# Conv-attention megakernel: the Fourier step's order in layer 0, and the last image's feed-forward with layer 1's norm behind it and its last group in halves

## The chip, the cores and the metric

The kernel runs on one core of one Trainium2 chip. The core has five engines, each with a queue of its own that is worked off in order: PE (TensorE, matmuls into PSUM), ACT (ScalarE), DVE (VectorE), POOL (GpSimd) and SP, which here only issues DMAs. The time is device microseconds of one execution; the number compared is the median of several executions. Lower is better.

## The reference

Eight images of 256 channels and 32 x 32 pixels, all float32, go through two layers. Layer 0 is a convolutional attention block followed by a feed-forward with a Fourier filter; layer 1 treats the pixels as 1024 tokens: causal attention, then eight experts with dense gates. Only the parts that the change touches are shown.

```python
def _edffn(x, pi_w, dw_w, fft_p, po_w):          # layer 0's feed-forward
    x = _conv1x1(x, pi_w)                        # 256 -> 1024 channels
    x = _dwconv3(x, dw_w)                        # 3 x 3 taps per channel
    x1, x2 = (x[:, :hid], x[:, hid:])            # hid = 512
    x = gelu(x1) * x2
    x = _conv1x1(x, po_w)                        # 512 -> 256 channels
    xp = x.reshape(B, Cc, gh, PS, gw, PS).transpose(0, 1, 2, 4, 3, 5)   # 8 x 8 blocks
    xf = jnp.fft.rfft2(xp) * fft_p
    xp = jnp.fft.irfft2(xf, s=(PS, PS))
    return xp.transpose(0, 1, 2, 4, 3, 5).reshape(B, Cc, Hp, Wp)

def _forward(x, ...):                            # layer 0
    a = _attention(_ln(x, norm1_w, norm1_b), ...)
    x = x + gamma1 * a
    f = _edffn(_ln(x, norm2_w, norm2_b), pi_w, dw_w, fft_p, po_w)
    return x + gamma2 * f

t = t + _L1_attn_ref(_ln_t(t), WQ, WK, WV)       # layer 1, attention
t = t + _L1_ffn_ref(_ln_t(t), ...)               # layer 1, experts
```

## The kernel before

Channels lie on the 128 partitions, so an image is two channel groups of 1024 pixels. All instructions of layer 0 and layer 1 go through recorders (class `InOrder`, line 73 in the profile's rows) that keep each engine's queue in the order in which the Python code issues them. Nothing is reordered later: what stands early in an engine's queue and is not ready holds up what stands behind it. Only the DMAs issued with `nc.sync` are free.

**Layer 0 is staggered over the images.** While image i's attention runs (`main_of(i)`, mostly PE and ACT), the taps of the feed-forward of image i-1 run on DVE (`hidden(i-1, ...)`), and at the opening of `main_of(i)` image i-2 gets its Fourier step (`spectrum(i-2)`). The function `level` weaves the two by costs: after each yield of the main list it issues side steps, in the main taps of 128 x 1024, until the summed DVE cost reaches a share of the summed PE cost (0.95 for images 2 to 6, 1.05 for image 7). The first 16 side steps of an image are the taps `o` of its own position encoding (`v_conv`), for which ACT first writes the middle tap (`v_middle`).

**The Fourier step** works on four bands of 256 pixels. For each band, `first` mixes 512 channels to 256 on PE (`pz`, eight matmuls that the profile counts as sixteen, since each is done in two passes) and ACT copies the result (`zf`); `second` is the product with the Fourier basis (`pf`) and, on DVE, the filter (`gf`); `third` is the product back (`py`) and two DVE additions into the image (`t`). I number them by band: pz 0, pf 0, gf 0, py 0, t 0 and so on; the two halves of the norm's output are xn 0 and xn 1. Before, a round of the loop issues `first(n)`, then `second(n-1)`, then `third(n-2)`, with a yield after each.

**The norm before the feed-forward** (`norm2`, `rms_norm`) is woven into that step: squares on ACT, their sums on PE (`ms`), the level on ACT (`yr`), a transpose (`tpy`), the factors on POOL, five empty steps, a transpose back (`tr`, then ACT's `rT`), and for each half a product that spreads the factors (`rbn`) and two DVE products (`xn`). `xn` is the input of the next group's opening `ph`. Then come the attention's scores `s` (product, ACT's `pT`, products `po` and `sums`).

The PSUM tiles `ms`, `tpy`, `tr`, `rbn`, `pf`, `py`, `pp` and `ph` share two banks (`ps_m`, tag `mm`); a new tile waits until an older one has been read.

**The last image** has no attention beside it. After `main_of(7)` the code runs, by hand order: the Fourier step of image 6 with the rest of image 7's attention (`ends`, `project`, product `pp`) and norm, woven with layer 1's first norm of image 0 (`norm0`, function `layer_norm`: transposes `tpt`, statistics on DVE, a chain on POOL, scalings of `zt_e` on ACT, transposes back `tpz`, copies `z_e`). Then the feed-forward of image 7 (`hidden(7, (), (2,), alone=True)`): eight channel groups of 128, of which group 2 runs its taps as products on PE (`pc`) and seven run them on DVE, eight taps each besides ACT's middle one. Groups 0 to 3 (`x`) go through gelu and are multiplied with groups 4 to 7 (`conv`) to `hid`; each such product is mixed at once (`mix`, into four `pz` tiles held over the whole image). Beside it, weighted by `together`, run 26 empty steps (`LEAD`) and then layer 1's keys and values of image 0 (`pk`, `pv`). At the end `spectrum(7)` runs alone, and layer 1 begins with the scores `s<-kk_e,z_e`.

Of the kernel before, what the change touches and what calls it, by code (L numbers as in the profile page):

```python
# [18 lines left out]
P = 128  # L19
# [7 lines left out]
PS = 8  # L27
# [78 lines left out]
def conv_attn_hybrid_kernel(  # L106
# [471 lines left out]
    with ExitStack() as l0:  # L578
# [484 lines left out]
        def hidden(b, lead, on_pe=(), alone=False):  # L1063


            opening = cur = None
            on_dve = [n for n in range(2 * ng) if n not in on_pe]
            for i, us in enumerate(lead):
                if opening is None and i >= 6 and b in ready2:
                    opening = open_group(b, 0, hpad[0])  # L1070
                    cur = next(opening)
                    next(opening)
                    opened = i
                elif opening is not None and i == opened + 2:
                    next(opening)

                yield us
            while b not in ready2:
                yield None
            if opening is None:  # L1080
                opening = open_group(b, 0, hpad[0])
                cur = next(opening)
                next(opening)
                opened = 16
            if opened > 13:
                next(opening)
            hid = hid_of[b] = {"h": {}, "out": [], "gelu": 0, "alone": alone}
            others = [(g, 3 * i) for i, g in enumerate(on_pe)]
            beside = {}
            for g, at in others:  # L1090

                beside[at + 1, 1], beside[at + 1, 6], beside[at + 2, 6] = g, g, g
            running = {}
            for m, n in enumerate(on_dve):
                pad, dst = cur
                for i, k in enumerate(OTHERS):
                    if m + 1 < len(on_dve):
                        if i == 3:
                            opening = open_group(b, on_dve[m + 1], hpad[(m + 1) % 2])
                            cur = next(opening)  # L1100
                            next(opening)
                        if i == 5:
                            next(opening)
                    if (m, i) in beside:
                        g = beside[m, i]
                        if g not in running:
                            running[g] = group_on_pe(b, g)
                        next(running[g])
                    tap(dst, pad, dw_w[:, n, :], k)
                    yield 1.3  # L1110
                hid["h"][n] = dst
                complete(b)

        def complete(b):

# [26 lines left out]
                gate(b)  # L1142
                yield 0.0

        def mix(b, g):

            pzs = mixed.setdefault(b, [])
            if not pzs:
                pzs += [ps_s.tile([P, 2, 2, C], F32, tag="s", name="pz") for _ in range(2)]
            for n in range(4):  # L1150
                for k in range(2):
                    blk = hid_of[b]["out"][g][:, (2 * n + k) * P : (2 * n + k + 1) * P]

                    pe.matmul(
                        pzs[n // 2][:, n % 2, k, :], blk, pow_[:, g, :], start=(g == 0 and k == 0), stop=(g == ng - 1 and k == 1)
                    )
# [3 lines left out]
        def spectrum(b):  # L1160

            hid = hid_of[b]["out"]
            nb = H // PS

            def first(n):
                if b in mixed:
                    pz = mixed[b][n // 2][:, n % 2]
                    z = two.tile([P, 2, C], F32, tag="ev", name="zf", bufs=3)
                    act.copy(z, pz)
                    return z  # L1170
                pz = ps_s.tile([P, 2, C], F32, tag="s", name="pz")
                for k in range(2):
                    for g in range(ng):
                        blk = hid[g][:, (2 * n + k) * P : (2 * n + k + 1) * P]
                        pe.matmul(pz[:, k, :], blk, pow_[:, g, :], start=(g == 0), stop=(g == ng - 1))
                z = two.tile([P, 2, C], F32, tag="ev", name="zf", bufs=3)
                act.copy(z, pz)
                return z

            def second(z):  # L1180
                pf = ps_m.tile([P, 2, C], F32, tag="mm", name="pf")
                pe.matmul(pf, dft, z, start=True, stop=True)
                gf = two.tile([P, 2, C], F32, tag="ev", name="gf", bufs=3)
                dve.tensor_mul(gf, pf, filt.unsqueeze(1).to_broadcast([P, 2, C]))
                return gf

            def third(n, gf):
                py = ps_m.tile([P, KC, PS, 2, W // 2], F32, tag="mm", name="py")
                for g in range(KC):
                    for k in range(2):  # L1190
                        pe.matmul(py[:, g, :, k, :], gf[:, k, g * P : (g + 1) * P], idft, start=True, stop=True)
                for g in range(KC):
                    tb = t[b][:, g, n * BAND : (n + 1) * BAND]
                    dve.scalar_tensor_tensor(
                        tb, py[:, g].rearrange("p r k c -> p (r k c)"), col("gam2", g), tb, ALU.mult, ALU.add
                    )

            z, gf = {}, {}
            for n in range(nb + 2):
                if n < nb:  # L1200
                    z[n] = first(n)
                    yield 3.5
                if 1 <= n <= nb:
                    gf[n - 1] = second(z.pop(n - 1))
                    yield 0.9
                if n >= 2:
                    third(n - 2, gf.pop(n - 2))
                    yield 0.9
            nc.sync.dma_start(t_d[b], t[b])
            if b + 3 < B:  # L1210
                load_x(b + 3)
# [16 lines left out]
        def silent(steps, n=None):  # L1228
            for _ in itertools.islice(steps, n):
                pass  # L1230
# [9 lines left out]
        def main_of(i):  # L1240

            steps = attend(i)
            if i >= 1:
                if i == 1:
                    second = norm2(i - 1)
                    silent(steps, 1)
                    silent(project(i - 1, (1,)))  # L1250
                    silent(second, 2)
                    v_middle(i)
                    yield from weave(second, steps, 2, rest=False)
                else:
                    mixing, second = spectrum(i - 2), norm2(i - 1, 5)
                    silent(second, 1)
                    silent(mixing, 1)
                    silent(project(i - 1, (1,)))
                    silent(second, 1)
                    v_middle(i)  # L1260
                    yield from some(mixing, 1)
                    yield from some(second, 1)
                    yield from some(mixing, 1)
                    yield from weave(second, mixing, 1, rest=False)
                    yield from weave(mixing, steps, 2, rest=False)
            yield from weave(steps, later_on(3, queries_keys(i + 1)) if 1 <= i < B - 1 else none(), 1)
            gelus = gelu_steps(i - 1) if i >= 1 else none()
            if i + 1 < B:
                stack(i + 1)
                steps, ends = values(i + 1), finish(i)  # L1270
                yield from some(gelus, 2)
                yield from some(steps, 2)
                yield from gelus
                yield from some(ends, 1)
                yield from project(i, (0,))
                yield from some(steps, 2)
                yield from some(ends, 1)
                yield from some(steps, 1)
                yield from ends
                yield from steps  # L1280
            else:
                yield from gelus
                yield from some(finish(i), 1)
                yield from project(i, (0,))
# [69 lines left out]
        silent(ends)  # L1354
        silent(mixing, 2)
        silent(project(B - 1, (1,)))
        head = weave(weave(second, mixing, 1), norm0, 1)
        while not ready2.get(B - 1):
            next(head)

        def rest():
            yield from head
            yield from itertools.repeat(1.0, LEAD)
            for us in keys0:
                yield 2.5 * us

        together(rest(), hidden(B - 1, (), (2,), alone=True), 1.0)
        for _ in spectrum(B - 1):
            pass


# [698 lines left out]
```

## Time and profile before

| | before |
|---|---|
| median of three executions | 3064.48 us (3064.29 to 3064.49) |
| profiled execution: time | 3065.18 us |
| profiled execution: span | 3063.5 us |
| PE busy | 2913.9 us (95%) |
| DVE busy | 2339.7 us (76%) |
| ACT busy | 1621.6 us (53%) |
| POOL busy | 317.1 us (10%) |
| mean granted clock of PE | 0.979 |
| layer 1's first scores | at 1353.46 us |

The span is that of the profiled execution, from its first to its last instruction. A row of the timeline gives start, duration, engine, line, operation, output and inputs, the number of merged instructions, and in square brackets the idle time of that engine just before and what ended it. A row of the windows gives the stretch, its length, and for PE, PE's weight loads, DVE, ACT and POOL the busy time with the number of instructions; then the granted clock of PE (1.00 is full), the DMA share and GB/s. A row of the waits gives who waited for whom, the total in us, the number of times and the longest.

### The profile page before, as it was taken

The numbers are of one execution on the slowest core, as the hardware profiler recorded it, in microseconds if no ns is written. First come the engines' busy times: TensorE is split into PE (matmuls) and PEld (weight loads), VectorE is DVE, ScalarE is ACT, GpSimd is POOL, SyncE is SP. The second block draws the span as 40 slices with busy tenths as digits, with TensorE's granted clock in tenths as the row PEclk, the third lists the DMA queues.
The fourth block names the chain that finished last, engine by engine and source line by source line (L and its number), as shares of the span: only waits on it lengthen the run. The fifth ranks groups of instructions, "written<-read, shape, count | busy, mean of one in ns | idle before, by whom it ended". The sixth has DMA issues, their size and how long they took to land.

```text
span 3063.5 us, 41588 instructions
## 1 busy us (share of the span) xinstructions
PE 2913.9 (95%) x16802; PEld 1923.7 (63%) x16802; DVE 2339.7 (76%) x2886; ACT 1621.6 (53%) x2440; POOL 317.1 (10%) x453
## 2 busy tenths in 40 slices
PE   7989999999999989889999999999999999999998
PEld 4644655555555555456666666677777777777775
DVE  2378888888888878776566654688988988888887
ACT  2555554545454535434444443565666666666664
POOL 1011111111111110011222222000000000000000
PEclk8999999999999989999999999999999999999999
DMA  6203030303030301003333311421211251122210
GB/s 196 48 10 83 28 84 28 83 29 83 29 83 29 83 15 35 16 35 128 131 133 122 126 78 69 165 83 49 90 69 69 97 186 69 69 76 90 76 69 29
DMA packets 63856, 234.87 MB, mean 77 GB/s; under 512 B 5590, under 2 KB 13862, under 8 KB 54822
## 3 DMA queue, kind: packets, MB, share of 16 engines
q1 hardware_dynamic: 63654, 232.12, 23.1%
q8 instruction: 134, 2.20, 0.3%
q14 instruction: 68, 0.56, 0.1%
HBM read 140.61 MB, written 91.49 MB: 76 GB/s over the span
## 4 chain that ended last, share of the span: by engine, by line
PE 74%; DVE 14%; ACT 6%; POOL 2%; DMA 2%; issue 2%; SPq 0%; ACTq 0%; DVEq 0%; POOLq 0%
PE pm L73 12%; PE pa L73 11%; PE q L73 11%; PE po L73 9%; PE s L73 6%; PE ph L73 6%; PE pq L73 3%; DVE conv L73 3%; PE sums L73 3%; DVE o L73 3%; DVE x L73 2%; ACT zt_e L73 2%; PE pz L73 2%; PE pv L73 2%; PE pp L73 2%
## 5 line engine op out<-in xcount | busy, mean ns | idle before, releaser
L73 PE MATMUL pa<-ze,w 128*128 128x512 f32 x1488 | 423.2, 393 | 0.0
L73 DVE SCALAR_TENSOR_TENSOR x<-hpad,vec,x 128x1024 f32<-128x1024 f32 x248 | 316.8, 1283 | 68.4 <-ACT x L73 60.9
L73 DVE SCALAR_TENSOR_TENSOR conv<-hpad,vec,conv 128x1024 f32<-128x1024 f32 x256 | 327.4, 1283 | 9.7 <-ACT conv L73 3.6
L73 PEld LDWEIGHTS pa<-ze,w 128*128 128x128 f32 x1488 | 278.4, 188 | 63.3 <-issue 3.3
L73 ACT ACTIVATE h<-pa,bn_o,s1a 128x512 f32<-128x512 f32 x256 | 198.6, 776 | 202.1 <-PE pa L73 202.1
L73 ACT ACTIVATE pT<-s 128x1024 f32<-128x1024 f32 x256 | 247.6, 1024 | 84.4 <-PE s L73 84.3
L73 PE MATMUL po<-pT,vT 128*32 128x256 f32 x4096 | 271.9, 383 | 0.0
L73 PE MATMUL q<-h2p,w 128*128 128x512 f32 x768 | 270.1, 460 | 0.1
L73 DVE SCALAR_TENSOR_TENSOR h<-pa,s1b,h 128x512 f32<-128x512 f32 x256 | 191.6, 748 | 96.4 <-PE pa L73 87.7
L73 PE MATMUL ph<-xn,piw 128*128 128x512 f32 x512 | 238.9, 608 | 13.4 <-ACT vpad L73 6.9
L73 PE MATMUL pm<-h,w 128*128 128x512 f32 x512 | 242.0, 595 | 0.0
L73 PE MATMUL q<-z_first,w 128*128 128x512 f32 x768 | 216.0, 390 | 2.8 <-DVE z_first L73 1.7
L73 PE MATMUL pm<-h1p,w 128*128 128x512 f32 x768 | 216.1, 389 | 0.5 <-DVE h1p L73 0.5
L73 PEld LDWEIGHTS q<-h2p,w 128*128 128x128 f32 x768 | 144.8, 189 | 84.3 <-issue 60.1
L73 DVE SCALAR_TENSOR_TENSOR o<-vpad,pe_w,o 128x1024 f32<-128x1024 f32 x128 | 164.0, 1283 | 26.1 <-ACT o L73 22.9
L73 PE MATMUL s<-qst,kst 128*128 128x256 f32 x1024 | 172.2, 311 | 8.9 <-ACT pT L73 6.3
L73 PEld LDWEIGHTS po<-pT,vT 128*32 128x32 f32 x4096 | 120.1, 110 | 84.4 <-issue 2.8
L73 PEld LDWEIGHTS ph<-xn,piw 128*128 128x128 f32 x512 | 92.3, 192 | 127.5 <-issue 99.5
L73 PEld LDWEIGHTS q<-z_first,w 128*128 128x128 f32 x768 | 143.8, 188 | 34.1 <-DVE z_first L73 2.9
L73 PEld LDWEIGHTS s<-qst,kst 128*128 128x128 f32 x1024 | 136.3, 193 | 45.2 <-issue 28.8
L73 PEld LDWEIGHTS pm<-h1p,w 128*128 128x128 f32 x768 | 144.1, 188 | 31.6 <-DVE h1p L73 0.9
L73 PE MATMUL sums<-pT,ones 128*32 128x256 f32 x2048 | 157.6, 379 | 0.0
(281 smaller groups left out, 5105.8 us busy)
## 6 DMA issues: line engine op xcount, KB each, us to landing
ze<-zd SPq DMA_DIRECT2D x29, 1536.0 KB, 6.4
qst<-part SPq DMA_DIRECT2D x32, 512.0 KB, 9.5
kst<-part SPq DMA_DIRECT2D x32, 512.0 KB, 16.4
te<-ud SPq DMA_DIRECT2D x32, 512.0 KB, 4.1
wd<-parts_w SPq DMA_DIRECT2D x20, 768.0 KB, 3.7
w<-wd SPq DMA_DIRECT2D x20, 768.0 KB, 5.7
zd<-parts SPq DMA_DIRECT2D x14, 1024.0 KB, 3.8
ud<-te SPq DMA_DIRECT2D x18, 512.0 KB, 3.4
```

Of the source, the lines that this page charges most:

```text
L73: return self._tc.keep_in_program_order(method(*args, **kwargs))
```

## The change

Three edits, all in layer 0's function body.

In `spectrum`, a round of the loop issues `second(n-1)` ahead of `first(n)`, and in `main_of(i)` for images 2 to 7 one more step of that list (now the product and filter of band 0) is taken without a yield, behind the norm's first sums and ahead of `v_middle`.

In the last image, only the first 12 of the 18 steps of `norm0` are woven into the head; the six that scale and transpose back follow at the start of `rest`, after the feed-forward's first group has been opened and its first tap issued by `next(feed)`. `LEAD`'s empty steps, keys and values follow behind them.

The last DVE group of the last image goes through the new `last_group`: its taps, products and mixing run on pixels 0 to 511 and then on 512 to 1023, and four steps of the image's Fourier step (bands 0 and 1: copy, product, filter) are issued between the taps of the second half. `mix` gets an argument for the halves.

```diff
@@ hidden @@
             for m, n in enumerate(on_dve):
                 pad, dst = cur
+                if alone and m == len(on_dve) - 1:
+                    yield from last_group(b, n, pad, dst)
+                    break
                 for i, k in enumerate(OTHERS):
...
+        def last_group(b, n, pad, dst):
+
+
+            hid, g, nb = hid_of[b], n - ng, H // PS // 2
+            assert len(hid["out"]) == g == ng - 1 and hid["gelu"] == ng
+            prod = two.tile([P, N], F32, tag="hid", name="hid", bufs=ng + 1)
+            hid["out"].append(prod)
+            blocks = prod.rearrange("p (n r k c) -> p k n r c", r=PS, k=2, c=W // 2)
+            a, b2 = (x.rearrange("p (n r k c) -> p k n r c", r=PS, k=2, c=W // 2) for x in (hid["h"][g], dst))
+            for h in range(2):
+                part = dst[:, h * HALF : (h + 1) * HALF]
+                for i, k in enumerate(OTHERS):
+                    src = inside(pad, h * (H // 2) + k // 3, k % 3, H // 2)
+                    dve.scalar_tensor_tensor(rows(part), src, dw_w[:, n, k : k + 1], rows(part), ALU.mult, ALU.add)
+                    if h == 1 and i in (1, 2, 4, 6):
+                        next(ending)
+                    yield 0.7
+                ns = slice(h * nb, (h + 1) * nb)
+                for k in range(2):
+                    dve.tensor_mul(blocks[:, k, ns], a[:, k, ns], b2[:, k, ns])
+                mix(b, g, (h,))
...
-        def mix(b, g):
+        def mix(b, g, halves=(0, 1)):
...
-            for n in range(4):
+            for n in (2 * h + i for h in halves for i in range(2)):
@@ spectrum @@
             for n in range(nb + 2):
+                if 1 <= n <= nb:
+                    gf[n - 1] = second(z.pop(n - 1))
+                    yield 0.9
                 if n < nb:
                     z[n] = first(n)
                     yield 3.5
-                if 1 <= n <= nb:
-                    gf[n - 1] = second(z.pop(n - 1))
-                    yield 0.9
                 if n >= 2:
                     third(n - 2, gf.pop(n - 2))
                     yield 0.9
@@ main_of @@
                     silent(mixing, 1)
                     silent(project(i - 1, (1,)))
                     silent(second, 1)
+                    silent(mixing, 1)
                     v_middle(i)
@@ behind the loop over the images @@
-        head = weave(weave(second, mixing, 1), norm0, 1)
+        head = weave(weave(second, mixing, 1), some(norm0, 12), 1)
         while not ready2.get(B - 1):
-            next(head)
+            next(head, None)
+        feed = hidden(B - 1, (), (2,), alone=True)
+        next(feed)
 
         def rest():
             yield from head
+            yield from norm0
             yield from itertools.repeat(1.0, LEAD)
             for us in keys0:
                 yield 2.5 * us
 
-        together(rest(), hidden(B - 1, (), (2,), alone=True), 1.0)
-        for _ in spectrum(B - 1):
+        ending = spectrum(B - 1)
+        together(rest(), feed, 1.0)
+        for _ in ending:
             pass
```

More of the change, by code (lines that the diff above doesn't have):

```diff
@@ L1112, in hidden @@
                 complete(b)
+        def last_group(b, n, pad, dst):
[3 more added lines that the diff above has]
+            hid["out"].append(prod)
+            blocks = prod.rearrange("p (n k r c) -> p k n r c", r=PS, k=2, c=W // 2)
+            a, b2 = (x.rearrange("p (n r k c) -> p k n r c", r=PS, k=2, c=W // 2) for x in (hid["h"][g], dst))
[11 more added lines that the diff above has]
+                mix(b, g, (h,))
         def complete(b):
```

## The prediction

> **What bounds the kernel now.** I read the page first, then TensorE's waits in layer 0, then the order of time of one image's opening and of the last image.
>
> ```profile
> PE 74%; DVE 14%; ACT 6%; POOL 2%; DMA 2%; issue 2%; SPq 0%; ACTq 0%; DVEq 0%; POOLq 0%
> ```
>
> The chain that ended last is three quarters TensorE: time given back to PE counts unless another engine holds the same stretch. TensorE's waits between 150 and 1320 us are led by the wait that the edit aims at:
>
> ```profile
> PE py L73 <- DVE gf L73: 24.0, 11, 4.8
> ```
>
> Is it PE's time to win? Here is VectorE, then PE, at the opening of image 4 (images 2 to 6 are alike):
>
> ```profile
> 617.01 10.53 DVE L73 SCALAR_TENSOR_TENSOR o<-vpad,pe_w,o 128x1024 f32<-128x1024 f32 x8 [2.05 <-ACT o L73]
> 627.46 0.68 DVE L73 TENSOR_TENSOR gf<-pf,filt 128x512 f32<-128x512 f32 x1
> 628.06 3.92 DVE L73 SCALAR_TENSOR_TENSOR o<-vpad,pe_w,o 128x1024 f32<-128x1024 f32 x3
> 631.89 0.68 DVE L73 TENSOR_TENSOR gf<-pf,filt 128x512 f32<-128x512 f32 x1
> 632.49 0.87 DVE L73 SCALAR_TENSOR_TENSOR t<-py,vec,t 128x256 f32<-128x256 f32 x2
> 633.28 2.60 DVE L73 SCALAR_TENSOR_TENSOR o<-vpad,pe_w,o 128x1024 f32<-128x1024 f32 x2
> ...
> 638.09 0.87 DVE L73 SCALAR_TENSOR_TENSOR t<-py,vec,t 128x256 f32<-128x256 f32 x2
> ```
>
> ```profile
> 623.54 1.02 PE L73 MATMUL pf<-zf,dft 128*128 128x512 f32 x2
> 628.20 2.08 PE L73 MATMUL py<-idft,gf 128*128 128x128 f32 x8 [3.64 <-DVE gf L73]
> 630.07 5.32 PE L73 MATMUL pz<-pow__152,hid 128*128 128x256 f32 x16
> ...
> 637.13 0.38 PE L73 MATMUL tr<-ident,r 128*8 128x128 f32 x2
> ...
> 642.97 1.20 PE L73 MATMUL s<-qst,kst 128*128 128x256 f32 x8
> ```
>
> The reader is to see that VectorE idles under 0.6 us from 617.01 until the last xn (start 641.94): 14 taps of 1.31 (8, 3, 2 and 1), four gf of 0.6, the t and xn pairs. PE waits 3.64 us because gf stands behind eight taps, yet it reaches s only when VectorE has worked through the list. The wait is cover for a chain on VectorE. The gap also costs clock; the granted clock (third figure from the end) in stretches of 3.41 us:
>
> ```profile
> 623.30:626.71 3.41, 1.26 (x4) 0.38 (x2) 3.30 (x4) 0.58 (x1) 3.16 (x4) 1.00 0.00 0
> 626.71:630.12 3.41, 1.92 (x9) 1.92 (x10) 3.38 (x4) 0.00 (x0) 1.28 (x3) 0.50 0.00 0
> 776.90:780.31 3.41, 1.38 (x5) 0.50 (x3) 3.30 (x4) 0.58 (x1) 3.16 (x4) 1.00 0.00 0
> ```
>
> Image 5 had the same gap and kept its clock (last line): from its first tap to s it took 25.45 us, image 4 took 25.96. So half clock cost only 0.5 there.
>
> **Images 2 to 6.** No instruction is added. The extra silent step puts pf 0 before pz 1, and its gf before all taps: PE 615.1 to 616.0, gf 616.2 to 616.8, inside the 2.05 us in which VectorE waits for ACT's middle taps anyway. That takes 0.6 from VectorE's chain; without the cover it would be late by 0.6. The pacing (costs written in the code) still emits 14 taps before the last xn, now as 8, 3, 3: gf0, 8 taps, gf1, 3 taps, t0, gf2, 3 taps, t1, gf3, t2, xn, t3, xn. Two things move against it. (1) PE runs pf 3 ahead of tr. PSUM has two banks for these tiles, so the third in the row py 1, pf 3, tr waits for t1, and behind tr stand the rest of the row and s. (2) Both t2 and t3 now stand ahead of the xn that followed them, and t2 must wait for a py that PE can start only after gf3; before, xn 0 filled that time.
>
> By the rows: gf1 at 627.46, t0 at 631.89, gf2 at 632.7, three taps, t1 at 637.1. PE: pf 1 at 620.4, pz 2 to 624.9, py 0 to 625.9, wait 2.3 for gf1, pf 2, pz 3 to 632.5, py 1, pf 3 to 634.8, then 3.4 us idle until t1 gives its bank back at 638.1 (1.02 after its start). At full clock: py 2 at 638.65, t2 639.75, xn 640.55, py 3 640.8, last rbn 642.1, s 642.5: 0.45 earlier than 642.97. At half clock (py pair to t 2.12 instead of 1.10, rbn to xn 1.15 instead of 0.69, as at 1103 us in image 7): t2 640.8, xn 641.7, py 3 641.8, last rbn 643.7, s 644.5: 1.5 later, and s to po takes 3.9 (334.90 to 338.79) instead of 3.4: +2.0.
>
> Which clock? The Trainium skill, page "TensorE: Matmul & The Clock Gate", Part 1, says that the clock halves after an idle window of about 3.4 us and comes back after a busy one. Read literally, a gap of 3.4 hardly ever covers a whole free-running window: full clock, -0.45 an image. This trace decides otherwise: 3.64 halved it in four of five images, and 3.17 us at 1326.7 did too (14 pz in 5.76). A stretch with 1.26 us of matmuls led to 0.50, one with 1.38 did not; I put the limit near 40% busy. The new gap is followed by sparse work (py, rbn), so I take half clock three times in four: 0.75 x 2.0 - 0.25 x 0.45 = +1.4. Four images: +5.6. Image 2 already ran s at half clock (333 to 336 us), so only +1.1.
>
> **Image 7** has share 1.05: nine taps first. Its row ran at half clock from 1101 to 1111 and reached s at 1108.31. After: t1 at 1099.15, plus the same 7.4 of the half-clock chain: 1106.6, -1.7. Layer 0's images: +5.6 + 1.1 - 1.7 = **+5.0**; bounds -7 (full clock everywhere) and +13 (below). PE is busy throughout the middles of images 3 to 6, so a shift of s is passed on. The DMAs td and the next x leave SP one step earlier, and nothing waits for them; POOL's factors, done at 628.1, stay ahead of tr in both orders.
>
> **The last image.**
>
> ```profile
> 1255.86 31.42 DVE L73 SCALAR_TENSOR_TENSOR x<-hpad,vec,x 128x1024 f32<-128x1024 f32 x24 [5.62 <-ACT x L73]
> 1302.57 10.53 DVE L73 SCALAR_TENSOR_TENSOR conv<-hpad,vec,conv 128x1024 f32<-128x1024 f32 x8 [2.74 <-ACT conv L73]
> 1328.07 10.52 DVE L73 SCALAR_TENSOR_TENSOR conv<-hpad,vec,conv 128x1024 f32<-128x1024 f32 x8
> 1346.00 0.69 DVE L73 TENSOR_TENSOR gf<-pf,filt 128x512 f32<-128x512 f32 x1 [6.08 <-PE pf L73]
> ```
>
> ```profile
> 1268.17 5.49 PE L73 MATMUL ph<-xn,piw 128*128 128x512 f32 x8 [6.88 <-ACT vpad L73]
> 1339.37 5.74 PE L73 MATMUL pz<-pow__152,hid 128*128 128x256 f32 x16 [5.40 <-DVE hid L73]
> 1353.46 1.98 PE L73 MATMUL s<-kk_e,z_e 128*128 128x512 f32 x4
> ```
>
> Layer 1 starts at 1353.46. Three terms. *Opening*: one pz (3.46) moves behind the projection, one pf (0.86) with a copy wait (0.9) before it: the projection comes 1.1 earlier. Sixteen transposes tpz and their waits (1.34 + 0.81) leave the path, so ph starts at 1247.5 instead of 1250.83; first tap 1252.6 instead of 1255.86, 3.3 earlier; minus 0.4 for a one in five chance that the now sparser PE opens at half clock (2 us): 2.9. The moved work (eight scalings of 0.51, four copies of 0.58, 6.4 on ACT, with 2.9 for group 1) fits beside the first group's 10.4 us of taps; if it did not, the second group would wait the excess, and gelu and vpad behind it on ACT. *Keys and values*: they start six taps later against the feed, so a pk no longer precedes group 4's second half and the last pv falls in PE's idle time after group 7. The stalls 0.69, 2.74 and 0.20 shrink to about 1.4: 2.2 won. The last group starts about 1323.0 instead of 1328.07: **5.1**. *Halves*: a tap of 512 elements is not in this trace; the nearest, xn's 128x512, is spaced 0.70 (bounds 0.65, half of 1.31, and 0.75, the t row): 16 x 0.70 + four short products of 0.38 = 12.7 instead of 11.8. gf0 stands in the tap queue and waits for mix, copy and pf: 1.4 at full clock, up to 4 at half, with the remaining taps and the last mix behind it. After the last product, eight pz instead of sixteen and half the spectrum remain, at half clock after a PE gap of 4.4. From the last group's start to layer 1: 26.0 instead of 25.4 (bounds 24 and 29). Tail: 5.1 - 0.6 = **-4.5** (bounds -7 and 0).
>
> **Sum.** The profiled execution is 3065.18 (span 3063.5 and 1.7 around it), 0.7 above the median. 3065.2 + 5.0 - 4.5 = 3065.7; taken from the median, **3065**.
>
> **Rivals.** (a) *PE keeps its clock* (the rule read literally; image 5 speaks for it, 3.17 at 1326.7 against): four images -0.45, image 2 -1.3 (0.8 at s, 0.5 in s), image 7 -3.7 (t1 plus 5.4), tail -5.1: 3053. Chance 0.18. (b) *Slower: the half clock after tr costs what it cost in image 7*, 8.38 from tr to s against 5.84 in image 4, with 0.5 on s: 3.0 - 0.45 = +2.6 in each of five images, nothing won in image 7, tail -4.5: 3073. It decides from 2.1 an image. Chance 0.17. (c) *The tail wins nothing* because gf0 stalls the taps at half clock or PE stays the limit to group 7: 3069.5. Chance 0.15. (d) *The waits vanish in full*: 5 x 3.64 + 4.84 = 23, tail 4.5: 3037. VectorE's row without idle time speaks against it: 0.03. My forecast: 0.47, own range 3061 to 3069.
>
> 0.2% (6.1 us) is about what a measurement tells from no change. Faster: (a), (d) and 0.04 of the forecast's edge; slower: (b) and 0.01. The range 3056 to 3072 leaves out (d), and about half of (a) and of (b).
>
> **What would show it.** After: py's wait for gf gone, pf waiting for gf about 2.3 and tr for t 3 to 3.4 in each image; gf before the first tap; s within 2 us of its old distance from the first tap; clock 0.50 around tr. Last image: first tap some 3 us sooner, last group about 5, and a wait of gf for pf inside the second half's taps. I am wrong if s comes over 3 us sooner per image (VectorE was not the bound) or if tr does not wait.

## The result and the profile after

| | before | after |
|---|---|---|
| median, six executions of each | 3064.39 us (3062.28 to 3069.32) | 3077.58 us (3074.67 to 3082.48) |
| ratio | | 1.0042 (95%: 1.0031 to 1.0054) |
| profiled execution: time, span | 3065.18, 3063.5 us | 3074.67, 3072.9 us |
| first o tap of image 2 to s of image 7 | 799.68 us | 811.44 us |
| from there to the last group's start | 219.76 us | 213.89 us |
| from there to layer 1's first scores | 25.39 us | 29.52 us |
| from there to the end of the span | 1710.0 us | 1709.3 us |

The changed kernel is 13 us slower; 3065 was predicted. The marks in the last four rows are read from the timelines of VectorE (DVE) and TensorE (PE). An image's s is the first row of scores behind its norm (image 7's, at 1108.31 us before, is what the recorded texts call the last s); the last group's start is the first tap of the last image's last DVE group. The marks say where the loss lies: +11.8 in the images, -5.9 up to the last group, +4.1 behind its start. That is 10 of the 13 us: after's profiled execution is the fastest of its six, and some 3 us of the medians' difference stand in no mark. After's waits of PE between 150 and 1320 us, longest total first (who waits for whom; total, times, longest):

```profile
PE tr L73 <- DVE t L73: 14.9, 6, 3.2
PE pf L73 <- DVE gf L73: 14.8, 6, 3.5
```

Before, py's wait for gf led with 24.0. Of it 0.3 is left, and 29.7 us of two other waits stand in its place. After's timeline of PE at image 4's opening, whose first o tap is now at 621.33:

```profile
629.28 1.05 PE L73 MATMUL py<-idft,gf 128*128 128x128 f32 x8
632.60 1.10 PE L73 MATMUL pf<-zf,dft 128*128 128x512 f32 x2 [2.27 <-DVE gf L73]
633.54 5.30 PE L73 MATMUL pz<-pow__152,hid 128*128 128x256 f32 x16
638.68 1.05 PE L73 MATMUL py<-idft,gf 128*128 128x128 f32 x8
639.57 1.12 PE L73 MATMUL pf<-zf,dft 128*128 128x512 f32 x2
642.44 0.38 PE L73 MATMUL tr<-ident,r 128*8 128x128 f32 x2 [1.75 <-DVE t L73]
...
648.29 2.08 PE L73 MATMUL s<-qst,kst 128*128 128x256 f32 x8
650.63 2.14 PE L73 MATMUL s<-qst,kst 128*128 128x256 f32 x8 [0.26 <-ACT pT L73]
652.70 1.73 PE L73 MATMUL po<-pT,vT 128*32 128x256 f32 x16
...
656.09 3.70 PE L73 MATMUL ph<-xn,piw 128*128 128x512 f32 x8
```

PE's idle time has moved from ahead of a py with a full pz behind it to ahead of tr, behind which stand only short products of few columns and then s and po. The windows of the same kernel (stretch, its length, busy time of PE, PE's loads, DVE, ACT, POOL with counts, then the granted clock) show what that does:

```profile
640.32:643.73 3.41, 1.54 (x10) 0.90 (x10) 2.57 (x4) 0.86 (x2) 0.00 (x0) 1.00 0.00 0
643.73:647.14 3.41, 3.39 (x16) 2.90 (x14) 2.28 (x4) 0.79 (x1) 0.00 (x0) 0.52 0.00 0
647.14:650.56 3.42, 3.23 (x13) 2.70 (x12) 3.04 (x5) 1.01 (x2) 0.00 (x0) 0.50 0.46 192
650.56:653.97 3.41, 3.34 (x20) 2.44 (x24) 1.73 (x2) 2.87 (x4) 0.00 (x0) 0.50 0.44 125
653.97:657.38 3.41, 3.41 (x43) 1.69 (x36) 0.00 (x0) 0.00 (x0) 0.00 (x0) 0.98 0.74 303
```

The clock is at 0.50 for three stretches, over the norm's end, s, ACT's wait and po (its changes lie 0.12 us behind the edges shown, hence 0.52 and 0.98). From s to the first ph image 4 takes 7.80 us (648.29 to 656.09). Before, it took 6.15, from 642.97 to this row:

```profile
649.12 3.70 PE L73 MATMUL ph<-xn,piw 128*128 128x512 f32 x8
```

In the last image, after's DVE and PE:

```profile
1332.91 1.29 DVE L73 TENSOR_TENSOR hid<-x,conv 128x512 f32<-128x512 f32 x2
1334.12 7.86 DVE L73 SCALAR_TENSOR_TENSOR conv<-hpad,vec,conv 128x512 f32<-128x512 f32 x8
...
1342.69 2.32 DVE L73 SCALAR_TENSOR_TENSOR conv<-hpad,vec,conv 128x512 f32<-128x512 f32 x3
1348.03 0.69 DVE L73 TENSOR_TENSOR gf<-pf,filt 128x512 f32<-128x512 f32 x1 [3.02 <-PE pf L73]
1348.64 3.11 DVE L73 SCALAR_TENSOR_TENSOR conv<-hpad,vec,conv 128x512 f32<-128x512 f32 x4
```

```profile
1342.49 2.75 PE L73 MATMUL pz<-pow__152,hid 128*128 128x256 f32 x8 [3.22 <-DVE hid L73]
1345.92 3.78 PE L73 MATMUL pf<-zf,dft 128*128 128x512 f32 x4 [0.68 <-ACT zf L73]
1353.52 3.51 PE L73 MATMUL pz<-pow__152,hid 128*128 128x256 f32 x8 [3.82 <-DVE hid L73]
...
1363.64 1.98 PE L73 MATMUL s<-kk_e,z_e 128*128 128x512 f32 x4
```

The half taps are 0.98 us apart in the first half, and in the second gf stands 3.02 us among them, waiting for a pf that PE runs at half clock after 3.22 us of idle time.

### The profile page after: what moved, and what is told of

The parts are those of the page before. It is cut to its first block, busy times and chain, and to the rows that moved or that the text cites. A ratio compares the mean times of both kernels' runs of the same rounds, so it can differ in the third digit from the quotient of the medians.

```text
span 3072.9 us, 41619 instructions
## 1 busy us (share of the span) xinstructions
PE 2925.4 (95%) x16802; PEld 1932.1 (63%) x16802; DVE 2342.7 (76%) x2896; ACT 1621.4 (53%) x2440; POOL 315.2 (10%) x453
## 4 chain that ended last, share of the span: by engine, by line
PE 74%; DVE 15%; ACT 6%; POOL 2%; issue 2%; DMA 1%; SPq 0%; ACTq 0%; DVEq 0%; POOLq 0%
PE pm L73 13%; PE pa L73 12%; PE q L73 11%; PE po L73 9%; PE s L73 7%; PE ph L73 6%; DVE o L73 3%; DVE conv L73 3%; PE pq L73 3%; PE sums L73 3%; DVE x L73 2%; ACT zt_e L73 2%; PE pv L73 2%; PE pp L73 2%; PE pz L73 1%
## 5 line engine op out<-in xcount | busy, mean ns | idle before, releaser
L73 DVE SCALAR_TENSOR_TENSOR conv<-hpad,vec,conv 128x1024 f32<-128x1024 f32 (+1 forms) x264 | 330.6, 1256 | 8.1 <-ACT conv L73 1.8
L73 PE MATMUL s<-qst,kst 128*128 128x256 f32 x1024 | 178.7, 320 | 6.4 <-ACT pT L73 3.8
L73 PEld LDWEIGHTS s<-qst,kst 128*128 128x128 f32 x1024 | 142.9, 202 | 42.2 <-issue 28.2
L73 ACT ACTIVATE hpad<-ph,pi_o 128x512 f32<-128x512 f32 x126 | 86.8, 689 | 137.5 <-PE ph L73 137.5
```

Source lines behind the costliest of these rows:

```text
L73: return self._tc.keep_in_program_order(method(*args, **kwargs))
```

## The experiments

Executions of one kernel spread over 3 to 15 us, in parts that no edit touches too: image 2's first tap lies between 307.9 and 313.7 us, and the stretch behind layer 1's start takes 1705.1 to 1710.3. So beside the median stands what the profiled execution took from image 2's first o tap to layer 1's first s. In the table, "image" is the mean distance between the first o taps of images 2 to 7.

| kernel | median us (n) | ratio to before, 95% | image | s of image 7 to last group | on to layer 1 | image 2 to layer 1 |
|---|---|---|---|---|---|---|
| before | 3064.39 (6) | | 153.84 | 219.76 | 25.39 | 1044.83 |
| after | 3077.58 (6) | 1.0031 to 1.0054 | 156.57 | 213.89 | 29.52 | 1054.85 |
| img_only | 3077.23 (9) | 1.0021 to 1.0040 | 157.07 | 218.61 | 25.46 | 1057.73 |
| img_fill | 3064.84 (13) | 0.9984 to 1.0000 | 153.50 | 220.04 | 25.68 | 1041.22 |
| img_fill_tr | 3066.48 (21) | 0.9994 to 1.0008 | 154.66 | 219.09 | 25.64 | 1047.38 |
| img_fill_pf | 3079.35 (5) | 1.0031 to 1.0059 | 156.56 | 218.25 | 25.39 | 1055.02 |
| after_fill | 3062.88 (13) | 0.9983 to 1.0003 | 153.51 | 214.27 | 29.19 | 1037.92 |
| swap_only | 3067.69 (13) | 0.9995 to 1.0012 | 154.87 | 218.50 | 25.89 | 1047.59 |
| before_fill | 3076.78 (8) | 1.0022 to 1.0043 | 156.18 | 220.83 | 25.64 | 1058.13 |
| before_fill2 | 3064.26 (14) | 0.9988 to 1.0004 | 153.72 | 224.04 | 25.65 | 1048.17 |
| tail_only | 3065.52 (22) | 0.9990 to 1.0003 | 153.74 | 216.21 | 29.19 | 1044.57 |
| norm_only | 3055.72 (7) | 0.9959 to 0.9981 | 153.84 | 211.98 | 26.52 | 1038.34 |
| norm_ahead | 3061.27 (13) | 0.9982 to 0.9998 | 153.83 | 211.63 | 26.65 | 1038.10 |
| norm_halves | 3063.17 (13) | 0.9983 to 1.0000 | 153.75 | 211.86 | 29.67 | 1040.83 |
| halves_late | 3059.74 (21) | 0.9976 to 0.9989 | 153.84 | 211.94 | 27.77 | 1039.55 |
| halves_only | 3064.78 (13) | 0.9990 to 1.0007 | 153.73 | 219.78 | 27.19 | 1046.13 |
| norm_fill | 3073.13 (10) | 1.0015 to 1.0034 | 155.96 | 211.99 | 26.59 | 1048.87 |
| norm_imgfill | 3056.43 (11) | 0.9965 to 0.9987 | 153.51 | 209.99 | 26.71 | 1031.15 |

The ratios stand to before as it ran in the same series; its medians there were 3066.30 (40 executions; img_only, tail_only, norm_only, img_fill), 3065.65 (33; before_fill, halves_only, swap_only, norm_fill), 3065.55 (40; norm_ahead, norm_halves, norm_imgfill, before_fill2) and 3065.91 (49; the other four). The added products of the fills repeat ones that are there, into the same place.

My theory after the result (A): the images lose by the half clock behind tr, and the halves take back what the norm's split wins. The rivals: (B) the order itself loses, by tr's wait for t1's bank and by t2 and t3 ahead of xn; (C) the tail loses.

### Which part loses

**img_only** is after with the norm unsplit and the last group whole, as before (the Fourier steps keep the new order in the last image too, as in the fills of it and in swap_only); **tail_only** is after with the old order in images 2 to 7:

```diff
 img_only
-        head = weave(weave(second, mixing, 1), some(norm0, 12), 1)
+        head = weave(weave(second, mixing, 1), norm0, 1)
...
-                if alone and m == len(on_dve) - 1:
-                    yield from last_group(b, n, pad, dst)
-                    break
 tail_only
-                if 1 <= n <= nb:
+                if ahead and 1 <= n <= nb:
...
-                    silent(mixing, 1)
                     v_middle(i)
```

> The new order of the Fourier steps and the extra step in images 2 to 7, the tail as before. Theory A (PE, stalled behind tr, runs at half clock through s and po in images 3 to 6): first o tap to s 1.0 to 1.7 us longer in images 2 to 6, s to the next image's first o tap 1 to 2 us longer in images 3 to 6, the last s of the images about 12 us later, time 10 to 13 us above before. Rival C (the loss is in the last image's halves): within 2 us of before.

> The whole change to the last image (norm split, last group in halves, new order of its Fourier steps), images 2 to 7 in the old order. Theory A: the tail by itself wins 1 to 3 us (last group starts 5 to 6 us sooner, last group's start to layer 1 grows from 25.4 to about 29.5), so 3061 to 3064. Rival C: 5 to 10 us above before.

With the images alone changed the kernel is 11 us slower (first tap to s 0.8 to 2.3 us longer, s to the next image's first tap 1.4 to 2.1); the tail, against A's 1 to 3 us, wins nothing that can be measured. Rival C falls.

### The clock or the order

**img_fill** gives PE work in both of its idle times of an image:

```diff
                 pe.matmul(pf, dft, z, start=True, stop=True)
+                for _ in range(3 if n == 3 and b < B - 2 else 0):
+                    tc.keep_in_program_order(nc.tensor.matmul(pf, dft, z, start=True, stop=True))
...
+                for g in [0, 1] * (2 if n == 0 and b < B - 2 else 0):
+                    for k in range(2):
+                        tc.keep_in_program_order(
+                            nc.tensor.matmul(py[:, g, :, k, :], gf[:, k, g * P : (g + 1) * P], idft, start=True, stop=True)
+                        )
```

> The images' new order as in img_only, with PE kept busy in both gaps of images 2 to 6: the two products py of band 0 are issued three times and pf of band 3 four times (the same products into the same place, no result changes). Theory A (half clock is the price): granted clock 1.00 around tr and s, first o tap to s near 25.5 us, s to the next first o tap as before, time 0 to 5 us below before. Rival B (the order is the price: the wait for t1's bank and t2, t3 ahead of xn): clock 1.00 as well, but the time stays 8 us or more above before.

Adding products that nobody needs, 4.7 us in each of six images (rows of 1.95 and 2.74), takes 12 us away. The half clock is the price; the order without it is level with before (0.9984 to 1.0000). Rival B falls. **after_fill** does the same in the whole changed kernel.

> The whole change, with PE kept busy in both gaps of images 2 to 6 as in img_fill (py of band 0 issued three times, pf of band 3 four times; no result changes). If the half clock of the images is the whole loss: clock 1.00 there, 153.5 us an image instead of 156.6, first o tap to s 25.7 us, 14 to 18 us less than the changed kernel from image 2's first tap to layer 1, time 3058 to 3065. If the changed order or the tail loses by itself: above 3070.

Image 4 of after_fill, timeline of PE (L1209 is the work added ahead of tr) and windows:

```profile
632.66 2.74 PE L1209 MATMUL pf<-zf,dft 128*128 128x512 f32 x6
636.05 0.38 PE L73 MATMUL tr<-ident,r 128*8 128x128 f32 x2 [0.65 <-DVE t L73]
636.56 1.16 PE L73 MATMUL py<-idft,gf 128*128 128x128 f32 x8
...
640.65 1.22 PE L73 MATMUL s<-qst,kst 128*128 128x256 f32 x8
```

```profile
636.91:640.32 3.41, 2.75 (x22) 2.36 (x21) 2.56 (x5) 1.22 (x1) 0.00 (x0) 1.00 0.00 0
640.32:643.73 3.41, 2.59 (x18) 2.11 (x18) 3.38 (x6) 2.30 (x3) 0.00 (x0) 1.00 0.65 257
```

tr still stands behind t1, but the clock stays at 1.00, the 128-column py takes 1.16 instead of 2.05 and s 1.22 instead of 2.08. First tap to s is 25.71 in each of images 2 to 6, s to ph 6.2, and the marks lie 16.9 us below after. **img_fill_tr** and **img_fill_pf** keep one of the two fills each (pf of band 3, or py of band 0).

> img_only with only the second gap filled (pf of band 3 issued four times, ahead of tr). If the idle time just ahead of tr starts the half clock that s and po run under, this alone takes most of the loss away: 153.5 to 154.5 us an image instead of 157.1. If the first gap (pf waiting for gf) starts it: 156 us or more.

> img_only with only the first gap filled (py of band 0 issued three times, ahead of the wait of pf for gf). If the gap ahead of tr is the cause, the clock still halves at tr: 156 to 157.5 us an image. If the first gap is the cause: 153.5 to 154.5.

Filling the gap ahead of pf alone brings 0.5 us an image (156.56) and nothing in the time (3079.35); filling the one ahead of tr brings 2.4 of the 3.6 us between img_only and img_fill. img_fill_tr's other 1.2 comes in four of its five images. In two of them (3 and 5) the open first gap still halves the clock for one stretch, some 11 us after the first tap; in the other two (2 and 6) the clock is at 0.50 for two stretches from 24 us on, around s, though tr waits only 0.65. Why it falls there, the run doesn't say.

**swap_only** is img_only without the extra silent step (its line taken out).

> img_only without the extra silent step: the new order in images 2 to 7, but tr issued ahead of pf 3 again and gf 0 behind the first taps. If the wait of tr for t1's bank starts the loss, that wait is gone, s comes 25 to 26.5 us after the first tap, and the time is within 3 us of before. If any new order loses because PE's idle time falls next to sparse work, the clock is 0.50 around tr and s all the same, and the time is 6 to 13 us above before.

tr's wait for t is gone, and rbn waits for t instead (13.2 us in six waits, up to 2.2). The loss shrinks to 1.0 us an image; the clock is 0.50 around s all the same. So both expectations hit in part: the extra silent step, which puts pf 3 ahead of tr and gf 0 ahead of the taps, makes about two thirds of the loss in the trace, and the time itself is not told from before.

### The old order, filled

**before_fill** gives PE work in the 3.64 us gap of the old order; **before_fill2** fills the gap ahead of tr as well, with py of band 1 three times.

```diff
                 pe.matmul(pf, dft, z, start=True, stop=True)
+                for _ in range(4 if n == 1 and b < B - 2 else 0):
+                    tc.keep_in_program_order(nc.tensor.matmul(pf, dft, z, start=True, stop=True))
```

> Before, with PE kept busy in its wait for gf: pf of band 1 is issued five times instead of once in images 2 to 7 (same product, same place, no result changes). Theory A (the wait is cover, only its clock costs): granted clock 1.00 through the opening, first o tap to s about 25.4 us in images 2 to 6, image 7 from 30.5 to about 26, s to the next first tap 0 to 1 us shorter; 4 to 9 us below before, about level with img_fill (both orders worth the same at full clock). Rival: the clock is irrelevant in the old order, within 1.5 us of before.

My expectation had the wrong sign: the kernel is 11 us slower. Windows and then PE of before_fill at image 4 (first o tap at 620.08):

```profile
636.66:640.07 3.41, 1.50 (x11) 1.04 (x10) 3.38 (x4) 0.00 (x0) 0.00 (x0) 1.00 0.00 0
640.07:643.48 3.41, 2.96 (x6) 1.43 (x6) 2.14 (x4) 1.64 (x2) 0.00 (x0) 0.50 0.00 0
643.48:646.90 3.42, 3.40 (x14) 2.93 (x14) 2.46 (x5) 0.00 (x0) 0.00 (x0) 0.50 0.00 0
```

```profile
639.69 0.38 PE L73 MATMUL tr<-ident,r 128*8 128x128 f32 x2 [1.91 <-DVE gf L73]
640.52 2.08 PE L73 MATMUL pf<-zf,dft 128*128 128x512 f32 x2 [0.45 <-ACT rT L73]
```

With its clock kept, PE came to tr early, idled there, and the half clock fell on the norm's end and s. Before, at the same place of image 4, the stretches that follow the prediction's are these:

```profile
630.12:633.53 3.41, 3.41 (x10) 2.69 (x10) 3.37 (x6) 0.00 (x0) 0.00 (x0) 0.50 0.00 0
633.53:636.94 3.41, 3.41 (x19) 2.73 (x17) 2.96 (x4) 0.58 (x1) 0.00 (x0) 1.00 0.00 0
```

The half clock fell on a pz in which PE had time to spare, and by tr (637.13) it was over; it cost 0.5 us (25.96 to s against 25.45 in image 5). before_fill loses by the mechanism of the change itself, without any new order.

> before_fill with the second gap filled too (py of band 1 issued three times ahead of tr; no result changes), old order. Theory A: before_fill lost 11 us because PE came to tr 1.9 us too soon and the half clock fell on tr, rbn and s; with that gap filled the clock stays 1.00 to s, first o tap to s 25 to 25.7 us, 153.3 to 153.8 us an image, 1 to 5 us below before and level with img_fill, so the order by itself is worth nothing at full clock. Rival (repeating products costs the time by itself, by queue or power): 8 us or more above before, as before_fill.

Filled twice, three of five images take 153.24 and the other two 154.4 and 154.5: at full clock the old order is no slower than the new one (153.50), and repeating products costs nothing that shows. The tail's 224.04 is outside the edit: the clock was 0.50 in the last image's opening, at 1250 us.

### The last image

**norm_only** is before with the norm's split alone (the last hunk of the change, with the old order and the whole last group).

> Before, with only the last part of the last image's norm put behind the opening; old order, last group whole. If the halves took back what the norm won (theory A), the last group starts 5 to 6 us sooner and keeps its 25.4 us to layer 1, so 4 to 6 us below before, and 2 to 4 below the kernel that has the whole tail change. Rival: PE is the limit behind the last group, the 5 us are lost to a longer wait there, and the time is within 1 us of before.

The gain is larger than expected: the last group starts 7.8 us sooner, 6.6 of it reach layer 1. The median says 10.6 (against 3066.30; its interval is 5.8 to 12.6), of which the marks show 6.5; in this profiled execution the stretch behind layer 1's start also took 4.9 less. The missing 1.1 is in this row of norm_only's DVE, 1.5 longer than before's (0.4 is got back behind it), beside POOL's work at the same time:

```profile
1320.06 12.06 DVE L73 SCALAR_TENSOR_TENSOR conv<-hpad,vec,conv 128x1024 f32<-128x1024 f32 x8
```

```profile
1319.62 3.50 POOL L1508 TENSOR_SCALAR_AFFINE_SELECT sel<-sel 32x1024 f32<-32x1024 f32 x2
```

Eight taps take 12.06 instead of 10.52, while POOL prepares layer 1's `sel`. Before, this work fell on the hid products of the group ahead:

```profile
1325.26 2.89 DVE L73 TENSOR_TENSOR hid<-x,conv 128x512 f32<-128x512 f32 x2
```

Elsewhere that row takes 1.29; the earlier group start moved POOL's work onto the taps. In all eighteen traces what stands beside `sel` takes 1.5 to 1.6 us more, be it hid, whole taps or half taps. That POOL slows VectorE is read from this coincidence, not from a run that takes POOL's work away; and a busy POOL alone doesn't do it, since in the prediction's first window POOL is busy 3.16 of 3.41 us with 128x8 operations beside taps of 1.31. The Trainium skill, page "GPSIMD Engine Reference", section "1. Specifications", names contention between GpSimd and DVE instructions with two inputs in SBUF; a tap has two.

**norm_ahead** adds the new order in the last image's opening alone (`spectrum(B - 2, True)`), **norm_halves** adds to norm_only the last group in halves, with the new order for its own Fourier steps, **halves_late** is norm_halves without the four `next(ending)` between the taps, and **halves_only** is before with the halves.

```diff
 halves_late, against norm_halves
-                    if h == 1 and i in (1, 2, 4, 6):
-                        next(ending)
                     yield 0.7
```

> norm_only, and besides it only the steps of image 6 that run in the last image's opening in the new order. If the new order is what made the opening of the full tail change 2.6 us slower than norm_only's (a whole pz of 3.6 us then lies between the projection and tr), the last s of image 7 to the first tap of the feed is 145.2 us instead of 142.6, the last group starts 2.5 to 4.5 us later than in norm_only, and the time is 2 to 5 us above norm_only. Rival (that difference was chance, by where the granted clock fell): 142.6 and level with norm_only.

In this trace the first tap comes 143.80 us after s of image 7 (142.63 in norm_only), but the second group no longer stalls, and the last group starts when it does in norm_only. The times speak for the expected loss all the same: the median is 5.5 us above norm_only's, and the two intervals don't overlap. So do the other traces: with this order and the split the last group starts at 211.63 (norm_ahead), 213.89 (after), 214.27 (after_fill) and 216.21 (tail_only), with the old order and the split at 209.99 to 211.99 (five kernels), a mean of 2.4 us sooner. tail_only differs from norm_halves in this order alone; its second group stalled 2.71 us, with the clock at 0.50 over a ph that took 3.55 us for the 1.88 in norm_ahead, and after_fill's stalled 2.70. It seems to matter where the half clock falls in the opening; a single trace of each can't say how often it falls there.

> norm_only, and besides it the last group in halves, with the new order for the last image's own Fourier steps. Theory A: last group's start as in norm_only (7 to 8 us sooner than before, counted from the last s of image 7), from there to layer 1 29 to 29.5 us instead of 26.5; 2 to 4 us above norm_only. As predicted (0.6 for the halves): within 1 us of norm_only.

> norm_halves with the last image's own Fourier steps put behind all its taps instead of between those of the second half. If gf's wait for pf in the tap queue is what makes the halves dear, last group's start to layer 1 falls from 29.7 to 27 or 28 us, still above the 26.5 of the whole group, because 16 half taps take longer than 8 whole ones. If the wait is cover for PE: 29.5 or more.

> Before, with only the last group in halves and the new order of the last image's own Fourier steps. Theory A: last group's start to layer 1 grows from 25.4 to 29 or 30 us (half taps 0.75 to 0.98 apart, PE idle twice for over 3 us, gf between the taps waiting 3 us for pf): 3 to 5 us above before. As predicted (halves cost 0.6): within 1.5 us of before.

In norm_halves the halves cost 3.15 us (29.67 against 26.52), in halves_late 1.25. So 1.9 is gf among the taps and 1.25 the sixteen half taps with the second mix, as the clock stood there. In the timeline of halves_late's DVE the second half has no gap:

```profile
1324.50 7.87 DVE L73 SCALAR_TENSOR_TENSOR conv<-hpad,vec,conv 128x512 f32<-128x512 f32 x8
1332.40 0.76 DVE L73 TENSOR_TENSOR hid<-x,conv 128x256 f32<-128x256 f32 x2
1333.08 6.25 DVE L73 SCALAR_TENSOR_TENSOR conv<-hpad,vec,conv 128x512 f32<-128x512 f32 x8
```

The first half's taps are 0.98 apart (beside POOL), the second's 0.78. In halves_only POOL's work still fell on the group before, and pf ran at full clock (1.98 us instead of 3.78 in after):

```profile
1329.84 6.32 DVE L73 SCALAR_TENSOR_TENSOR conv<-hpad,vec,conv 128x512 f32<-128x512 f32 x8
...
1340.49 0.69 DVE L73 TENSOR_TENSOR gf<-pf,filt 128x512 f32<-128x512 f32 x1 [1.31 <-PE pf L73]
```

There the halves cost 1.8 in all, gf included, and not the 3 to 5 expected; the total doesn't show it. So norm_halves's 3.15 is not all the halves' own: gf's wait is 2.89 there, with pf at half clock, and 1.31 here.

### Both gains together

**norm_fill** joins norm_only and before_fill, **norm_imgfill** joins norm_only's tail and img_fill's images.

> norm_only and before_fill together. Theory A: the two gains add, since one lies in images 2 to 7 and the other in the last image's opening: 13 to 19 us below before, 4 to 8 below norm_only. Rival (the time set free is taken back at layer 1, or the fill does nothing): as norm_only.

> norm_only's tail (whole last group, old order there) with img_fill's images (new order, both gaps filled by repeating products, no result changes). Theory A: the two gains add, 153.5 us from one image's first o tap to the next, tail as in norm_only: 8 to 14 us below before and at or below norm_only. Rival: the fill is lost again at the tail, then above norm_only.

norm_fill inherits before_fill's loss. norm_imgfill is 13.7 us shorter than before between the marks and 7.2 shorter than norm_only; by the median both beat before and after and can't be told from each other (the profiled execution of norm_imgfill started image 2 5.4 us later and took 3.7 more behind layer 1's start). Filling the gaps takes work of no use; norm_only is the plain improvement.

## Why the prediction was wrong

**What bounds the images: right for full clock.** There VectorE's list set s. With all waits left in the order and the clock at 1.00, first tap to s is 25.71 in the new order; before, image 5 at full clock had 25.45. Rival (d), the waits vanishing in full, was rightly small; the -0.45 predicted for full clock came out as +0.26.

**The waits: right.** pf waited 2.27 in image 4 (2.3 predicted); tr started 21.1 us after the first tap, as worked out, with t1 at 20.1. tr waited 1.75 there and up to 3.2 elsewhere, because image 4's first gap had already halved the clock and stretched a pz to 5.30.

**The half clock: the step that failed.** The prediction priced it at +2.0 us, and "s to po takes 3.9 instead of 3.4" let it end with s. First tap to s grew by 1.5, 1.5, 1.0, 1.4 and 1.7 in images 2 to 6, 7.1 in all, near the 1.5 that I had worked out for an image at half clock. But the clock stayed at 0.50 for three stretches (four in image 6), through po: s to the next image's first tap grew by 0.15, 1.02, 1.66, 2.01 and 1.74, 6.6 in all, and in image 4 all of it lies between s and ph. I had read the price off image 2, where before's half clock ended during s. I had also given a quarter of the weight to full clock, which none of images 2 to 6 had behind tr. Images: +11.8 for +5.0. Rival (b) had the size (2.6 an image; images 2 to 6 lost 2.7 each) and the cause, but by luck: it put the price between tr and s, at 8.38, and on s. tr to s took 5.7 to 6.7; the rest came from tr's later start, and half of the loss lay behind s.

**Image 7: right.** -1.9 between first tap and s; -1.7 predicted.

**Last image up to the last group: right as sums.** First tap 3.0 sooner (2.9), last group 5.9 sooner (5.1). That is luck in part. The split alone was worth 4.9 and 7.8 (norm_only), and the new order in the opening, counted as 1.1 won for the first tap, took about 1.9 of each away in after's trace.

**The halves: the term of the sum that was mis-sized.** +0.6 predicted, +4.1 measured, above the upper bound of 29 us. The half tap was 0.78 and not 0.70, above its bound of 0.75; gf stood 3.0 and not 1.4 in the queue, because the first half's taps leave PE idle for 3.22 us and the granted clock falls; and POOL's work moved onto the taps. By the runs: 1.1 for POOL (norm_only), 1.25 for half taps and second mix, 1.9 for gf among the taps. The last two hold for this clock: with PE idle for 0.94 us only (halves_only) gf waits 1.31, near the 1.4 that the prediction gave for full clock. The tail brought 1.7 us, not 4.5.

**The rule on the clock.** Against the literal reading (a whole idle window) the trace decided rightly. My own limit of near 40% busy is too neat: stretches with 0.37, 0.44 (before_fill) and 0.45 (after) recorded busy were followed by 0.50, one with 0.40 was not. In the eighteen traces, from 300 us to layer 1, every stretch of the clock's grid below 0.41 was followed by 0.50, but so were stretches up to 0.83 (before, from 329.7 us).

## What to carry to other kernels

Ask of every idle time of TensorE what runs just behind it: a half clock that falls on work with slack is nearly free (0.5 us here), the same half clock on a chain of short products is paid (2.7 us an image here), and it can outlast the products that one has in view (10 us and more here). Removing a wait moves the idle time to the next wait; find that place before pricing the removal. A split into halves pays for its instructions in each half (0.78 a half tap, 1.31 a whole one), and an operation that waits for another engine should not be put into a queue whose other entries are the critical ones.

## What was not expected of the hardware

The half clock outlived busy stretches: 3.39 and 3.23 us of 3.41 recorded busy, and the next stretch was still at 0.50 (after, image 4); before, in image 4, one stretch with 3.41 busy was enough, and in image 7 one with 3.41 (from 1101.14) was not. The rows there are products of few columns at half clock. The recorded busy time alone thus doesn't decide; what does, no run here settles. The changes of the clock lie on one grid of 3.413 us in each of the traces (37 changes before, none over 0.01 us off it). And 3.6 us of useless products in each of six images, in a gap where PE did nothing, made the kernel 11 us slower.
